# Moving half of a factor's sums into the end of the attention, and tying the residual adds to later products

## The chip, the cores and the metric

The kernel is one program for a Trainium2 chip and uses one of its cores. Its engines are TensorE (PE, matrix products, with the weight loads PEld), VectorE (DVE), ScalarE (ACT), GpSimd (POOL) and SyncE (SP, which here only starts transfers). Each works through its own queue of instructions in order and waits on semaphores for the others; transfers can be started from SP, ACT and POOL. PSUM is the memory that PE writes its results to, SBUF the working memory; DRAM holds the inputs, the outputs and intermediate results.

The metric is the device time of one execution in microseconds (us), the median of several runs. A profiled execution gives a trace beside it.

## The reference

Attention and a feed-forward network run side by side on the normalised input, and both are added to it. All is float32.

```python
def reference(x, Wq, Wk, Wv, Wo, w1_w, w1_s, w2_w, w2_s, h1_w, h1_s, h2_w, h2_s, w3_w, w3_s):
    # x: 2 x 2048 x 256; W*: 256 x 256; the *_w hold -1, 0 and 1, the *_s a scale for each output
    xn = layernorm(x)
    return x + attn(xn, Wq, Wk, Wv, Wo) + ffn(xn, ...)

def attn(x, ...):           # one head, causal, scores scaled by 256 ** -0.5
    return softmax(mask(x @ Wq @ (x @ Wk).T / 16)) @ (x @ Wv) @ Wo

def ffn(x, ...):            # tlin(x, w, s) = (x @ w.T) * s
    h = silu(tlin(x, w1_w, w1_s)) * tlin(x, w2_w, w2_s)     # 256 -> 1024
    h = gelu(tlin(h, h1_w, h1_s))                           # 1024 -> 1024
    h = gelu(tlin(h, h2_w, h2_s))                           # 1024 -> 1024
    return tlin(h, w3_w, w3_s)                              # 1024 -> 256
```

## The kernel before

**Blocks and precision.** The 4096 tokens make N = 8 blocks of TB = 512, blocks 0 to 3 of the first sequence and 4 to 7 of the second (NB = 4); a block has NT = 4 tiles of P = 128 rows. A float32 value goes into PE as a sum of two parts, high and low. `split_into` makes them: the high part is a rounding copy on ACT (L187), the low part a subtraction on DVE (L188).

**Attention.** It runs first. Row tiles (n, t) are taken in the order j = 0 to 31, sequence one from its last tile down, then sequence two upwards. Of each tile the scores are made (PE L425, moved out of PSUM by DVE L434, exponential on ACT L446), turned (DVE L308, to DRAM as d, back as e, both by SP), split into high and low parts pT (ACT L484; L486 on DVE, or on POOL for odd key blocks) and used to weigh the values (PE L518 and L523). The results r go to DRAM as `r_d`. The tiles of x lie in a pool `xp` of four buffers of 512 KB; for the second sequence they are last read when keys are made in the steps j = 13 to 24. `beside(cost)` is called between the steps and drops small pieces of other work among them (`looks`: loads of weights on ACT's queue, checks, the sums of the first square layer's factors on DVE).

**Feed-forward network** (`ffn_ternary`). It follows and works on pairs of blocks (n, n + 1). `first(n)` makes the gated layer: the products (PE L174), silu on ACT (L182), the second factor on DVE (L183). The two square layers, "h1" and "h2", are done as a Strassen-Winograd scheme: the hidden width is halved and the two blocks of the pair are the other half, so that seven products take the place of eight. `STEPS` names them, weight factor and right side:

```python
STEPS = [("A11", "B11"), ("S1", "T1"), ("S2", "T2"), ("S4", "B22"), ("S3", "T3"), ("A12", "B21"), ("A22", "T4")]
```

Each product is 32 matmuls (L883) of some 0.227 us. The right sides are sums of what the layer before gave, made in four chunks: T1 (L858) and T2 (L864) on DVE, the source of T3 (L863) and of T4 (L922) on POOL; each is then split. In the trace T1 and T2 are `h_T`, B22 is `h_B`, T3 is `q`, and the later B21 and T4 are `h_h_B` and `h_h_T` in the first layer of the first pair. L894 copies and L903 and L904 add up and apply gelu to what products left in the banks `ps` and `ps_own`.

**Factors.** The seven weight factors of a layer lie in DRAM (`factors`), and `fetch_factors` (SP, L998, 1 MB each) keeps three of them loaded ahead. A11, A12 and A22 are parts of the weights, S1 to S4 are sums of them, made by the kernel in four chunks. Those of h1 are made in the attention. Those of h2 are made while the first pair goes through the gated layer and its first square layer: `fetch_h2(c)` loads chunk c into one of two staging buffers (SP, L957), `make_h2(c)` makes its four sums in place on POOL (L963 to L966, 128x512 each) and stores them (POOL's queue, L967, 1 MB). `later` says at which point of the program each stands: fetches of chunks 0 and 1 ahead of everything, `make_h2(0)` and `make_h2(1)` in the gated layer, the fetches of chunks 2 and 3 there too, their sums behind products 2 and 3. `copy_h2` copies the unsummed parts from DRAM to DRAM, and `load_w3` (product 5) loads the last weights and rounds them on POOL.

**Residuals.** `rests_of(n)`, called behind product 3 of the second square layer, loads r and x of both blocks (SP L1013 and L1014) into the staging buffers and adds them on POOL, one add of 128x1024 for each block (L1015). The last product of the pair (PE L1044), its scaling and the store follow.

**What sets the order.** A scheduler in the tile framework lays the instructions of each engine in an order of its own from dependences, buffers and estimated times; program order is only a start. `tc.issue_after(mark)` tells it to place an instruction behind another in this plan; it is no data dependence.

Of the kernel before, what the change touches and what calls it, by code (L numbers as in the profile page):

```python
# [30 lines left out]
LEAST = 5  # L31
TURN_KEYS = [8, 10, 12, 14]
LOOKS_FROM = 3
LEAD = 2
# [31 lines left out]
def attn_ffn_kernel(  # L66
# [77 lines left out]
    def sums_of_factors(sums, halves, which, engine=nc.gpsimd):  # L144

        (a11, a21), (a12, a22) = ((t[:, :HB], t[:, HB:]) for t in halves)
        done = sums.bitcast(F32) if sums.dtype == F32R else sums
        for i in which:
            x, y, op = (
                (a21, a22, ALU.add),  # L150
                (done[:, 0, :], a11, ALU.subtract),
                (a12, done[:, 1, :], ALU.subtract),
                (a11, a21, ALU.subtract),
            )[i]
            engine.tensor_tensor(sums[:, i, :], x, y, op)


# [33 lines left out]
    with ExitStack() as actx:  # L191
# [476 lines left out]
        for i, (srcs, steps) in enumerate(items):  # L668
# [7 lines left out]
            if not nxt and i + 1 < len(items):  # L676
                looks.append((4000, lambda i=i: fetched_weights(i + 1)))

        since = [0]

        def beside(cost):
            if j >= LOOKS_FROM:
                since[0] += cost
                if looks and since[0] >= looks[0][0]:
                    since[0] = 0
                    looks.pop(0)[1]()
# [75 lines left out]
        while until < len(tiles) - 1:  # L762
# [16 lines left out]
            merged(a, b, beside)  # L779

        last_quarter = [bank(), bank()]
        with tc.issue_after(marks["PE"]):
            gated_products(last_quarter, xh0, HK - 1)

    def ffn_ternary(actx):
# [83 lines left out]
        def square(layer, n, B, sets, last, beside):  # L869
# [6 lines left out]
            def product(step, out, start):  # L876
# [3 lines left out]
                for o in range(HK):  # L880
                    for c in range(HK):
                        for a in range(2):
                            nc.tensor.matmul(  # L883
                                out=out[o], lhsT=w[:, c, ts(o, P)], rhs=sets[right][c][:, a, :],
                                start=(start and c == 0 and a == 0), stop=(c == HK - 1 and a == 1),
                                skip_group_check=True,
                            )
                if step in beside:
# [57 lines left out]
            return C, nxt  # L946

        raw_h2 = {}

# [9 lines left out]
        def make_h2(c):  # L959

            t = raw_h2.pop(c)
            a11, a21, a12, a22 = (t[:, i, :] for i in range(4))
            nc.gpsimd.tensor_tensor(a22, a21, a22, ALU.add)  # L963
            nc.gpsimd.tensor_tensor(a21, a11, a21, ALU.subtract)
            nc.gpsimd.tensor_tensor(a11, a22, a11, ALU.subtract)
            nc.gpsimd.tensor_tensor(a12, a12, a11, ALU.subtract)  # L966
            nc.gpsimd.dma_start(out=factors["h2"][:, 1:5, c, :], in_=t)  # L967
# [7 lines left out]
        def copy_h2(step):  # L975
# [4 lines left out]

        later = {
            "B11": lambda: make_h2(0), "B21": lambda: (make_h2(1), copy_h2(0)), "B12": lambda: fetch_h2(2),
            "B22": lambda: fetch_h2(3), 0: lambda: copy_h2(5),
            2: lambda: (make_h2(2), copy_h2(6)), 3: lambda: make_h2(3), 5: load_w3,
# [19 lines left out]
        def rests_of(n):  # L1004
# [4 lines left out]
            )  # L1009
            rests = {}  # L1010
            for i, m in enumerate((n + 1, n)):
                rests[m] = rest = rt[:, ts(i, NT), :]
                nc.sync.dma_start(out=rest, in_=r_d[m].rearrange("p (t d) -> p t d", d=D))  # L1013
                nc.sync.dma_start(out=xt[:, ts(i, NT), :], in_=rows_of(m))  # L1014
                nc.gpsimd.tensor_tensor(rest, rest, xt[:, ts(i, NT), :], ALU.add)  # L1015
            return rests

        load_xh(1)
        for c in range(2):
            fetch_h2(c)  # L1020
        fetch_factors()

        for n in range(0, N, 2):
# [6 lines left out]
            B, sets = square("h1", n, B, sets, False, later)  # L1030
            rests = {}
            B, sets = square("h2", n, B, sets, True, {3: lambda: rests.update(rests_of(n))})
            for m in (n + 1, n):
# [221 lines left out]
```

## Time and profile before

| | us |
|---|---|
| median of 3 runs | 869.92 |
| lowest and highest | 867.67, 871.22 |
| the profiled execution | 868.75 |
| its span in the trace | 866.9 |
| PE busy | 849.5 |
| DVE busy | 644.1 |
| ACT busy | 498.7 |
| POOL busy | 234.7 |

Of the profiled execution 1.85 us lie around the span. Mean granted clock of PE: 0.998. The feed-forward part starts at about 281 us, and the first pair's first square layer runs from 302 to 354.

In timelines a row is: start in us, duration in us, engine, line, operation, output <- inputs (names without buffer numbers), shape, count, and in brackets the idle time before it and who ended that. Rows of windows give, for each engine, busy us and instructions, in the order PE, PEld, DVE, ACT, POOL, then the granted clock of PE as a share of full speed, the busy share of the DMA engines, and GB/s.

### The profile page before, as it was taken

To read this page: it belongs to the slowest core of one execution; us is meant where nothing else is said; L and a number is where in the kernel's file an instruction comes from. 1 tells how busy PE (TensorE), PEld (TensorE's weight loads), DVE (VectorE), ACT (ScalarE), POOL (GpSimd) and SP (SyncE) were. 2 spreads that over 40 slices of the span, in tenths; PEclk is the share of its full clock that TensorE was granted. 3 is DMA by queue.
4 is the path that set the end of the run, shared out by engine and by line. 5 is a ranking of instruction groups with operands and counts; after the bars stand their busy time and mean duration, and the time that the engine had idled before them with its cause. 6 is when DMAs were issued, how large, how long until landed. Compare 5 with 4: busy or idle time off the path is not lost.

```text
span 866.9 us, 12257 instructions
## 1 busy us (share of the span) xinstructions
PE 849.5 (98%) x4298; PEld 720.5 (83%) x4298; DVE 644.1 (74%) x1123; ACT 498.7 (58%) x881; POOL 234.7 (27%) x178
## 2 busy tenths in 40 slices
PE   9999799999999999999999999999999999999997
PEld 7988688988888878878988888988888898888887
DVE  6689685887965799986596596479478648848764
ACT  3456665655655466676257576436557635557671
POOL 3022823111111666630142150026024003502300
PEclk9999999999999999999999999999999999999999
DMA  8987899667881998754234444433444431144411
GB/s 276 361 233 233 249 314 291 222 234 231 286 283 51 389 403 282 285 194 152 93 132 143 144 146 141 144 116 109 145 145 145 145 135 58 49 146 146 146 49 53
DMA packets 62678, 162.51 MB, mean 187 GB/s; under 512 B 6545, under 2 KB 36369, under 8 KB 53265
## 3 DMA queue, kind: packets, MB, share of 16 engines
q1 hardware_dynamic: 57792, 145.14, 48.6%
q10 hardware_dynamic: 3728, 12.32, 4.6%
q0 software_dynamic: 1088, 4.19, 1.3%
q8 instruction: 36, 0.59, 0.3%
q14 instruction: 34, 0.27, 0.1%
HBM read 120.21 MB, written 47.71 MB: 194 GB/s over the span
## 4 chain that ended last, share of the span: by engine, by line
PE 83%; DVE 6%; DMA 5%; issue 2%; POOL 1%; ACT 1%; SPq 1%; DVEq 0%; ACTq 0%; POOLq 0%
PE ps_own L883 22%; PE ps L883 21%; PE ps L425 7%; PE ps L174 6%; PE ps_own L174 6%; PE po L518 4%; PE ps_own L1044 4%; PE ps L1044 4%; PE ps L398 3%; DMA e<-d 3%; DMA d<-b 2%; PE po L523 2%; PE ps L382 1%; POOL x L345 1%; DVE h_T L188 1%
## 5 line engine op out<-in xcount | busy, mean ns | idle before, releaser
L425 PE MATMUL ps<-k,q 128*128 128x512 f32 (+3 forms) x480 | 109.0, 366 | 0.4 <-ACT q L264 0.4
L425 PEld LDWEIGHTS ps<-k,q 128*128 128x128 f32 x480 | 82.0, 189 | 13.4 <-ACT q L264 1.2
L518 PE MATMUL po<-v,pT 128*128 128x512 f32 x272 | 79.1, 401 | 6.5 <-ACT pT L484 4.7
L486 POOL TENSOR_TENSOR pT<-e,pT 128x512 fp32r<-128x512 f32 (+3 forms) x30 | 36.8, 1229 | 140.1 <-ACT pT L484 102.6
L1015 POOL TENSOR_TENSOR rt<-rt,xt 128x1024 f32<-128x1024 f32 x8 | 21.9, 2758 | 170.3 <-issue 114.8
L904 ACT ACTIVATE k_h_u<-k_h_u,h_s_sb 128x512 f32<-128x512 f32 x64 | 45.9, 723 | 36.6 <-DVE k_h_u L903 36.0
L446 ACT ACTIVATE s<-s,low 128x1024 f32<-128x1024 f32 (+7 forms) x48 | 42.9, 895 | 30.8 <-DVE low L440 30.6
L518 PEld LDWEIGHTS po<-v,pT 128*128 128x128 f32 x272 | 47.3, 189 | 14.3 <-ACT pT L484 5.5
L863 POOL TENSOR_TENSOR k_h_u<-k_h_p,k_h_u 128x512 f32<-128x512 f32 x16 | 23.3, 1459 | 122.1 <-ACT q L187 106.0
L484 ACT CAST pT<-e 128x512 fp32r<-128x512 f32 (+3 forms) x60 | 32.8, 574 | 38.8 <-DMA e<-d 26.9
L434 DVE TENSOR_SCALAR_CACHE_REDUCE s<-ps 128x512 f32<-128x512 f32 (+3 forms) x80 | 47.2, 598 | 5.0 <-PE pt L490 3.1
L523 PEld LDWEIGHTS po<-v,pT 128*128 128x128 f32 x272 | 42.4, 188 | 6.8 <-DVE pT L486 0.7
L523 PE MATMUL po<-v,pT 128*128 128x256 f32 x272 | 46.2, 283 | 0.1
L188 DVE TENSOR_TENSOR q<-k_h_u,q 128x512 fp32r<-128x512 f32 x32 | 43.4, 1384 | 0.0
L308 DVE STREAM_TRANSPOSE b<-s 128x1024 f32<-128x1024 f32 (+3 forms) x30 | 33.4, 1124 | 8.3 <-ACT s L446 4.8
L922 POOL TENSOR_TENSOR k_h_p<-f_h_B,k_h_p 128x512 f32<-128x512 f32 x16 | 32.6, 2065 | 20.0 <-DVE h_h_T L188 20.0
L174 PE MATMUL ps<-xh,w_sb 128*128 128x512 f32 x144 | 36.4, 391 | 0.8 <-ACT b L182 0.8
L863 POOL TENSOR_TENSOR f_w_B<-f_w_B,f_w_B 128x512 f32<-128x512 f32 x16 | 26.8, 1692 | 33.1 <-DVE f_w_B L183 33.1
L903 DVE TENSOR_TENSOR k_h_u<-ps_own,k_h_u 128x512 f32<-128x512 f32 x32 | 21.7, 686 | 17.5 <-PE ps_own L883 17.4
L904 ACT ACTIVATE k_h_p<-k_h_p,h_s_sb 128x512 f32<-128x512 f32 x32 | 22.8, 722 | 19.3 <-DVE k_h_p L903 19.3
L903 DVE TENSOR_TENSOR k_h_u<-ps,k_h_u 128x512 f32<-128x512 f32 x32 | 22.0, 690 | 14.3 <-PE ps L883 14.3
L174 PE MATMUL ps<-xh1t,w_sb 128*128 128x512 f32 x128 | 31.8, 389 | 0.0
(178 smaller groups left out, 2206.2 us busy)
## 6 DMA issues: line engine op xcount, KB each, us to landing
w_h_S<-factors_h SPq DMA_DIRECT2D x32, 1024.0 KB, 4.8
w_h_A<-factors_h SPq DMA_DIRECT2D x24, 1024.0 KB, 4.8
d<-b SPq DMA_DIRECT2D x18, 512.0 KB, 3.9
e<-d SPq DMA_DIRECT2D x72, 128.0 KB, 3.2
xT_d<-k SPq DMA_DIRECT2D x8, 1024.0 KB, 6.0
stg<-in_ffn_h_w ACTq DMA_DIRECT2D x16, 512.0 KB, 4.8
r_d<-r SPq DMA_DIRECT2D x8, 512.0 KB, 4.3
factors_h<-xh SPq DMA_DIRECT2D x4, 1024.0 KB, 4.5
```

Of the source, the lines that this page charges most:

```text
L174: nc.tensor.matmul(out=p, lhsT=w[:, c, ts(o, P)], rhs=xh[:, c, a, :], start=(c == 0 and a == 0), stop=(c == DC - 1 and a == 1),)
L188: nc.vector.tensor_tensor(r[:, 1, :], f, r[:, 0, :].bitcast(F32), ALU.subtract)
L425: nc.tensor.matmul(out=ps[:, :w], lhsT=qs[n][:, c, a, ts(t, P)], rhs=ks[m][:, c, b, :w], start=(k == 0), stop=(m < n and k == 3 * DC - 1),)
L434: marks["DVE"] = nc.vector.tensor_scalar(st["s"][:, ds(at, w)], ps[:, :w], 1.0, None, ALU.mult, ALU.max, accum_out=st["tops"][:, m - first ...
L446: marks["ACT"] = nc.scalar.activation(st["s"][:, at], st["s"][:, at], AF.Exp, bias=low, accum_out=st["sums"][:, u // UK : u // UK + 1],).ins
L518: nc.tensor.matmul(out=st["po"], lhsT=pT[:, 0, ts(j, P)], rhs=vs[m][:, j, :, :], start=(m == first and j == 0), stop=False,)
L523: marks["PE"] = nc.tensor.matmul(out=st["po"][:, 0, :], lhsT=pT[:, 1, ts(j, P)], rhs=vs[m][:, j, 0, :], start=False, stop=(m == n and j == ...
L863: nc.gpsimd.tensor_tensor(B["B12"][i], B["B22"][i], B["B12"][i], ALU.subtract)
L883: nc.tensor.matmul(out=out[o], lhsT=w[:, c, ts(o, P)], rhs=sets[right][c][:, a, :], start=(start and c == 0 and a == 0), stop=(c == HK - 1 ...
L903: nc.vector.tensor_tensor(r[o], banks[o], r[o], ALU.add)
L904: nc.scalar.activation(C[k][o], r[o] if r else banks[o], AF.Gelu, scale=s[:, at : at + 1])
L1044: nc.tensor.matmul(out=ys[t][:, :D], lhsT=h[c][:, a, ts(t, P)], rhs=w3_sb[:, c, :], start=(c == 0 and a == 0), stop=(c == HC - 1 and a == 1),)
```

## The change

Chunks 0 and 1 of h2's factor sums are made in the attention from tile j = 24 on: their weights are loaded into x's four buffers on ACT's queue, the eight sums are made one at a time on POOL between the attention's steps, and four stores of 512 KB follow on POOL's queue. The feed-forward part loads chunks 2 and 3 at its start, behind `xh1` and the first three factors. The residual adds are cut from two of 128x1024 to eight of 128x256 for each pair and are built inside `tc.issue_after` of the last matmul of product 3 (block n + 1) and product 4 (block n). The number and size of the sums stays the same.

```diff
+RAWS_FROM = 24
+EARLY = 2
...
+    def sums_in_place(halves):
+        a11, a21, a12, a22 = halves
+        return (
+            (a22, a21, a22, ALU.add), (a21, a11, a21, ALU.subtract),
+            (a11, a22, a11, ALU.subtract), (a12, a12, a11, ALU.subtract),
+        )
...
+        raws = {}
+        def fetch_raws(c):
+            raws[c] = [xp.tile([P, 2, HB], F32, tag="x", name=f"raw_h2_{c}_{i}") for i in range(2)]
+            for t, k in zip(raws[c], (c, c + HK)):
+                with tc.issue_after(marks["ACT"]):
+                    nc.scalar.dma_start(out=t, in_=h2[:, k, :].rearrange("p (i o) -> p i o", i=2))
+        def sum_raws(c, i):
+            with tc.issue_after(marks["DVE"]):
+                nc.gpsimd.tensor_tensor(*sums_in_place([t[:, k, :] for t in raws[c] for k in range(2)])[i])
+        def store_raws(c):
+            for i, t in enumerate(raws[c]):
+                nc.gpsimd.dma_start(out=factors["h2"][:, 1 + 2 * i : 3 + 2 * i, c, :], in_=t)
+        made_of_h2 = [(0, lambda c=c: fetch_raws(c)) for c in range(EARLY)]
+        for c in range(EARLY):
+            made_of_h2 += [(9000, lambda c=c, i=i: sum_raws(c, i)) for i in range(4)]
+            made_of_h2.append((4000, lambda c=c: store_raws(c)))
+        since_made = [0]
         def beside(cost):
+            if j >= RAWS_FROM:
+                since_made[0] += cost
+                if made_of_h2 and since_made[0] >= made_of_h2[0][0]:
+                    since_made[0] = 0
+                    made_of_h2.pop(0)[1]()
...
-                            nc.tensor.matmul(
+                            marks["PE"] = nc.tensor.matmul(
...
-                            )
+                            ).ins
...
-            a11, a21, a12, a22 = (t[:, i, :] for i in range(4))
-            nc.gpsimd.tensor_tensor(a22, a21, a22, ALU.add)
-            nc.gpsimd.tensor_tensor(a21, a11, a21, ALU.subtract)
-            nc.gpsimd.tensor_tensor(a11, a22, a11, ALU.subtract)
-            nc.gpsimd.tensor_tensor(a12, a12, a11, ALU.subtract)
+            for k in sums_in_place([t[:, i, :] for i in range(4)]):
+                nc.gpsimd.tensor_tensor(*k)
...
         later = {
-            "B11": lambda: make_h2(0), "B21": lambda: (make_h2(1), copy_h2(0)), "B12": lambda: fetch_h2(2),
-            "B22": lambda: fetch_h2(3), 0: lambda: copy_h2(5),
+            "B21": lambda: copy_h2(0), 0: lambda: copy_h2(5),
             2: lambda: (make_h2(2), copy_h2(6)), 3: lambda: make_h2(3), 5: load_w3,
         }
...
-                nc.gpsimd.tensor_tensor(rest, rest, xt[:, ts(i, NT), :], ALU.add)
-            return rests
+                adds[m] = [(r, r, xt[:, i * NT + t, :], ALU.add) for t in range(NT) for r in [rest[:, t, :]]]
+            return rests, adds
+        def add_rests(adds):
+            for k in adds:
+                with tc.issue_after(marks["PE"]):
+                    nc.gpsimd.tensor_tensor(*k)
         load_xh(1)
-        for c in range(2):
+        fetch_factors()
+        for c in range(EARLY, HK):
             fetch_h2(c)
-        fetch_factors()
...
-            rests = {}
-            B, sets = square("h2", n, B, sets, True, {3: lambda: rests.update(rests_of(n))})
+            rests, adds = {}, {}
+            def fetch_rests():
+                for a, b in zip((rests, adds), rests_of(n)):
+                    a.update(b)
+                add_rests(adds[n + 1])
+            B, sets = square("h2", n, B, sets, True, {3: fetch_rests, 4: lambda: add_rests(adds[n])})
```

More of the change, by code (lines that the diff above doesn't have):

```diff
@@ L779, in attn_ffn_kernel @@
             merged(a, b, beside)
+        assert not made_of_h2
         last_quarter = [bank(), bank()]
@@ L946, in square @@
             return C, nxt
+        marks = {}
         raw_h2 = {}
@@ L1030, in ffn_ternary @@
             B, sets = square("h1", n, B, sets, False, later)
-            rests = {}
-            B, sets = square("h2", n, B, sets, True, {3: lambda: rests.update(rests_of(n))})
+            rests, adds = {}, {}
+            def fetch_rests():
[3 more added lines that the diff above has]
+            B, sets = square("h2", n, B, sets, True, {3: fetch_rests, 4: lambda: add_rests(adds[n])})
             for m in (n + 1, n):
```

## The prediction

> **What bounds the kernel now.** The first view is the page's list of engines, the second its chain of waits by engine:
>
> ```profile
> PE 849.5 (98%) x4298; PEld 720.5 (83%) x4298; DVE 644.1 (74%) x1123; ACT 498.7 (58%) x881; POOL 234.7 (27%) x178
> ...
> PE 83%; DVE 6%; DMA 5%; issue 2%; POOL 1%; ACT 1%; SPq 1%; DVEq 0%; ACTq 0%; POOLq 0%
> ```
>
> TensorE (PE) is busy 98% of the span. The change neither adds nor removes a matmul, so it can only win back PE's waits or lengthen them. The third view lists those waits (us in total, times, longest):
>
> ```profile
> PE po L518 <- ACT pT L484: 4.7, 2, 2.6
> ...
> PE ps_own L883 <- DVE h_h_T L188: 1.4, 2, 1.0
> ...
> PE ps L174 <- ACT b L182: 0.8, 1, 0.8
> PE ps L883 <- DVE h_T L188: 0.7, 1, 0.7
> ...
> PE ps L883 <- DVE f_w_B L183: 0.3, 1, 0.3
> ```
>
> The first lies at 87 and 103 us, long before anything that the change touches. The rest is the prize. Taken as start-to-start gaps above the usual 0.227 us of a matmul they are 0.92 us at 261 (end of the attention), 0.41 at 307 and 0.85 at 318 (first pair, first square layer), 0.59 and 1.13 at 370 (second square layer). All of them together are 3.9 us of 867, so little can be won.
>
> The fourth view is the timeline of the first square layer, where the change moves most: PE, then VectorE (DVE), then GpSimd (POOL).
>
> ```profile
> 309.78 7.43 PE L883 MATMUL ps_own<-h_T,w_h_S 128*128 128x512 f32 x32
> 317.04 1.75 PE L883 MATMUL ps<-h_T,w_h_S 128*128 128x512 f32 x7
> 319.48 5.96 PE L883 MATMUL ps<-h_T,w_h_S 128*128 128x512 f32 x25 [0.69 <-DVE h_T L188]
> ```
>
> ```profile
> 316.44 2.98 DVE L188 TENSOR_TENSOR h_T<-f_w_B,h_T 128x512 fp32r<-128x512 f32 x3
> 319.35 4.69 DVE L188 TENSOR_TENSOR q<-f_w_B,q 128x512 fp32r<-128x512 f32 x4
> ...
> 329.67 7.21 DVE L188 TENSOR_TENSOR h_h_T<-f_w_B,h_h_T 128x512 fp32r<-128x512 f32 x4
> ...
> 379.09 2.48 DVE L188 TENSOR_TENSOR h_h_T<-k_h_p,h_h_T 128x512 fp32r<-128x512 f32 x4
> ```
>
> ```profile
> 317.20 5.09 POOL L922 TENSOR_TENSOR f_w_B<-f_w_B,f_w_B 128x512 f32<-128x512 f32 x3 [1.23 <-DVE h_T L188]
> 324.00 1.79 POOL L963 TENSOR_TENSOR stgt_h<-stgt_h 128x512 f32<-128x512 f32 x1 [1.71 <-DMA stgt_h<-in_ffn_h_w]
> ```
>
> Product 2 (its right side T2) ran 7 matmuls and waited until 319.42, when DVE had split the last chunk of T2 (the third h_T). Two readings carry the forecast. First, a DVE subtraction with both operands in SBUF takes 2.48/4 = 0.62 us when POOL is idle (at 379) and 7.21/4 = 1.80 us while POOL adds (at 329, beside the sums of L963). POOL next to it needs 5.09/3 = 1.70 us an operation. So DVE and POOL take turns: in a stretch where both have such work, one pair costs 1.70 us and DVE loses 1.1 us to each POOL operation. DVE's products from PSUM (L183, 0.74 us) show no such stretch. Second, T2 was only 0.85 us late, so any POOL operation set ahead of it on this path costs 1.1 us of PE.
>
> **Part 1, the first square layer.** Before, the sums of chunks 0 and 1 (8 POOL operations) ran from 288.9 to 302, those of chunks 2 and 3 from 324 on, after T2. After, chunks 0 and 1 are gone from here, but chunks 2 and 3 come from the first fetch of this stage, and in the built order their 8 sums are mixed with the four L863 (T3's source) and the first three L922 (T4's source), ahead of T2's last split. On DVE the order changes too: L188 of T2's chunk 3 now stands behind all four splits of T3 (q); before, T2's four came first. L922 of a chunk waits for T2's split of it, so POOL's delays and DVE's feed each other.
>
> When the sums start: SP issues its first transfer here at 280.5. The new queue is xh1t, three factor loads and chunk 2, 5.24 MB. This window carries
>
> ```profile
> 289.00:296.00 7.00, 7.00 (x32) 5.80 (x31) 5.95 (x7) 3.37 (x6) 6.84 (x5) 1.00 1.02 423
> ```
>
> 423 GB/s at a full DMA share (last two columns), so 12.4 us, and with some 3 us from issue to the first landing chunk 2 is there at 296. DVE then has 19 subtractions with both operands in SBUF up to and with T2's chunk 3 (the rest of T1, four splits of B22, four L864, four of T2, four of T3), POOL 15 operations. 15 pairs of 1.70 and four DVE operations alone at 0.60 are 27.9 us: from 296.9 to 324.8, where before PE went on at 319.5. That is **+5.3 us**. The same count over the old order (from 303.0: 7 POOL operations, 14 of DVE) gives 303.0 + 11.9 + 4.2 = 319.1 against 319.42 measured. Bounds: 1.80 a pair and six alone give 327.5 (+8); chunk 2 at 293, as chunk 1 landed before, and pairs partly apart give 321.5 (+2). PE would wait twice, some 2 us for T2's chunk 2 and some 3 to 5 us for chunk 3.
>
> Such waits can cost more than themselves. PE's timeline has one in the attention, and the row of windows behind it shows the clock:
>
> ```profile
> 138.44 1.19 PE L518 MATMUL po<-v,pT 128*128 128x512 f32 x3 [1.89 <-DVE r L537]
> ```
>
> ```profile
> 139.00:142.40 3.40, 3.40 (x16) 3.02 (x15) 1.88 (x6) 2.26 (x5) 0.00 (x0) 0.50 0.99 282
> ```
>
> After a wait of 1.89 us the granted clock (third column from the end) was 0.50 for 3.4 us; twelve matmuls of L398 took 2.88 us in it where their count at full clock is 1.54, so about 1.5 us were lost. After the waits of 2.2 and 2.6 us at 87 and 103 us there was no drop: one case in three. Two waits by 1/3 by 1.5 us: **+1.0** (0 to +3). [...]
>
> **Part 2, the second square layer.** PE's two waits at 370 (0.59 and 1.13) come from T2 there, split while POOL made the two adds of 128x1024 at 358.8 and 367.1; DVE's operation beside each took 2.9 us. After, this pair's adds stand in POOL's order right behind the rounding of w3 and ahead of L863 of this layer. Their rows can land by about 339 (SP's queue: r behind the rounding, x behind a factor load that is free when product 2 ends), so they are over near 345, and L863 is needed at 346 plus the 5 us that PE is later. The two waits go: **-1.7** (0 if the adds hold L863 up). Next late there is nothing: T2 gains 2 x 2.2 us against a lateness of 1.7.
>
> **Part 3, the adds cut in eight.** Two of 2758 ns become eight of 128x256. POOL's rows of that shape are 652 ns (L345, one input) and 1252 ns (L486), so 5.2 to 10 us against 5.5; I take the middle, as either way it is off the path: in later pairs POOL has been idle for tens of us before them. POOL's order holds no wait for PE at these adds, only for their rows, so "released by later products" sets a place in the queue and no time. Price **0** (-0.5 to +1).
>
> **Part 4, the attention's end.** Four loads of 512 KB on ACT's queue come at 187 to 190, and eight sums (1.3 to 1.7 us) and four stores (0.81 each, before two) on POOL between 196 and 210. In 190 to 195 the DMA share is 1.01 at 380 GB/s already, in 195 to 201 it is 0.90. 2.1 MB at 380 GB/s is 5.5 us, of which 0.6 find room: rows of e can come up to 4.9 us late. PE's order has scores put ahead of the weighing that needs them. Queued behind the sums on POOL is the low part of tile (5,2)'s pT: it is written at some 211.3, and PE asks for it at about 212. Five or so of DVE's operations lose 1.1 us there while it must clear score banks. I take 2.1 us lost (0 to 4.9), nearer to the low end because PE has a tile's scores in hand, less the 0.9 at 261, which the order of loads ahead of it can close: **+1.2** (-0.9 to +4).
>
> **Sum.** 5.3 + 1.0 - 1.7 + 0 + 1.2 = **+5.8 us**. On the profiled execution (868.75, span 866.9 and 1.85 around it) that is 874.6; that execution is 1.17 below the median of 869.92, so the median becomes **875.7**.
>
> **Rivals.**
> - A, not slower: POOL is free from the stage's start to 296 and only four DVE operations fall in that time today beside sums; if chunk 2 lands late enough, or T2's last split is written before PE's 7th matmul of product 2 at 317.9, all waits there and at 370 go: 0.85 + 0.41 + 1.72 = 3.0 us, 866.9. For it: eight POOL operations have left before 302. Against: 15 are queued ahead of T2's end instead of 7. It decides on whether POOL's sums run ahead of L863 or slip behind L922. Chance 0.22.
> - B, the attention's end is hit: e's rows come the whole 4.9 us late and POOL's pT after 213, 4 to 6 us on top, 880.5. For it: DMA share of 1.01. Against: 0.7 us of margin on pT. Chance 0.13.
> - C, the adds hold up L863 of the second layer: instead of -1.7 a wait of 1 to 3 us, 877 to 880. It decides if their rows land after 345. Chance 0.08, counted in the forecast's upper part.
>
> **How the numbers follow.** The forecast has 0.65. 0.5% is 4.35 us, about what a measurement of this kernel can tell from no change. Of the forecast's 0.65 about a quarter lies below +4.35 (its T2 term at +2 to +4); B is slower wholly; A is within the bound but for 0.04 of it. So faster 0.04, same 0.35, slower 0.61. The range runs from 868.0 (most of A's side left out) to 881.5 (T2's +8 with the attention at its value, or B). The forecast's own is 871.5 to 879.5.
>
> **What would show it.** Right: in the changed trace PE waits 5 to 7 us in all within product 2 of the first pair's first layer, for L188 of h_T; DVE's SBUF subtractions take 1.7 us from about 296 to 323; POOL's sums begin near 296; no PE wait in the second layer's T2. Possibly a row of granted clock 0.50 follows the wait. Wrong: that wait under 2 us, chunk 2 there before 293, or new PE waits of over 4 us between 190 and 262.

## The result, and the profile after

The change makes the kernel slower: 883.59 us (median of four executions, 880.12 to 885.69) against 868.79 for the kernel before in the same series, a ratio of 1.016 (95% interval 1.0132 to 1.0189). A second series, told below, gave 879.24 against 867.64, 1.0126 (1.0086 to 1.0165). So the cost is 11 to 15 us. 875.7 was forecast, with a range up to 881.5: the direction was right, and the forecast loss of 5.8 us is 40 to 50% of the measured one. The first series lies 2.1 us above the range, the second inside it. Further down, a bracket such as (1.016, 1.0132 to 1.0189) holds the ratio to the kernel before in the same series and its interval.

The profiled execution after took 880.12 us, span 878.3. The page's engines and its chain of waits:

```profile
PE 853.5 (97%) x4298; PEld 722.9 (82%) x4298; DVE 641.7 (73%) x1123; ACT 501.2 (57%) x881; POOL 241.6 (28%) x204
...
PE 70%; DMA 13%; DVE 10%; ACT 3%; issue 3%; SPq 1%; POOL 0%; DVEq 0%; ACTq 0%
```

PE's busy time rose by 4.0 us with the same 4298 matmuls, so part of the loss is not waiting but slower matmuls: the clock was at half in some stretches, and a matmul alone between two waits took 0.50 us (both below). In the chain DMA went from 5% to 13%. PE's waits:

```profile
PE po L528 <- ACT pT L494: 7.8, 4, 2.5
PE ps L922 <- DVE h_T L198: 4.6, 3, 2.2
...
PE ps L922 <- ACT h_T L197: 1.5, 2, 0.7
```

(L528 is L518 of before, L922 is L883, L198 and L197 are L188 and L187.) The wait of the second square layer for `h_h_T` is gone, the one for T2 (`h_T`) has become 6.1 us, and the attention's wait for pT went from 4.7 to 7.8 (the 4.7 and half of the 7.8 lie at 86 to 107 us, ahead of what the change touches).

To put a place to each microsecond, take the time between the starts of fixed matmuls in PE's order: 1000 to 1560 is the attention's end, 1560 to 1800 holds product 2 of the first square layer, 1800 to 2000 the first products of the second layer, 2000 to 4290 all the rest. Every kernel below does the same PE work in each (one profile each, us):

| kernel | attention's end | product 2's stretch | second layer | rest |
|---|---|---|---|---|
| before | 105.4 | 56.0 | 47.3 | 466.4 |
| after | 109.2 | 64.0 | 45.3 | 465.5 |
| after, second series (f4) | 112.8 | 64.6 | 45.3 | 465.6 |

After loses 3.8 to 7.4 us at the attention's end and 8.0 to 8.6 around product 2, and wins 2.0 in the second layer and 0.8 to 0.9 in the later pairs: 9 to 13 us. (Both profiles of after were also 2.1 us later at matmul 1000. From the first matmul to that one the kernels told here took 182.3 to 188.8 us, kernels without the change among the shortest and the longest, so I take these 2.1 us as variation.)

**Product 2** in PE's timeline after, to be held against the prediction's three lines:

```profile
322.36 0.84 PE L922 MATMUL ps<-h_T,w_h_S 128*128 128x512 f32 x3
323.55 0.50 PE L922 MATMUL ps<-h_T,w_h_S 128*128 128x512 f32 x1 [0.35 <-DVE h_T L198]
324.80 0.50 PE L922 MATMUL ps<-h_T,w_h_S 128*128 128x512 f32 x1 [0.75 <-ACT h_T L197]
327.51 0.50 PE L922 MATMUL ps<-h_T,w_h_S 128*128 128x512 f32 x1 [2.21 <-DVE h_T L198]
328.76 0.80 PE L922 MATMUL ps<-h_T,w_h_S 128*128 128x512 f32 x1 [0.75 <-ACT h_T L197]
331.60 7.81 PE L922 MATMUL ps<-h_T,w_h_S 128*128 128x512 f32 x25 [2.04 <-DVE h_T L198]
```

Five waits, 6.10 us in all: for the low part (L198) of T2's chunk 1 and for the high (L197) and low parts of chunks 2 and 3. DVE and POOL at that time:

```profile
314.72 5.66 DVE L198 TENSOR_TENSOR h_B<-f_w_B,h_B 128x512 fp32r<-128x512 f32 x2
...
327.38 0.68 DVE L903 TENSOR_TENSOR f_w_B<-f_w_B,b 128x512 f32<-128x512 f32 x1
327.98 2.96 DVE L198 TENSOR_TENSOR q<-f_w_B,q 128x512 fp32r<-128x512 f32 x3
330.86 0.68 DVE L198 TENSOR_TENSOR h_T<-f_w_B,h_T 128x512 fp32r<-128x512 f32 x1
```

```profile
301.98 8.19 POOL L1003 TENSOR_TENSOR stgt_h<-stgt_h 128x512 f32<-128x512 f32 x5 [26.14 <-DMA stgt_h<-in_ffn_h_w]
...
316.04 1.30 POOL L902 TENSOR_TENSOR f_w_B<-f_w_B,f_w_B 128x512 f32<-128x512 f32 x1
317.28 1.30 POOL L1003 TENSOR_TENSOR stgt_h<-stgt_h 128x512 f32<-128x512 f32 x1
318.53 1.28 POOL L902 TENSOR_TENSOR f_w_B<-f_w_B,f_w_B 128x512 f32<-128x512 f32 x1
```

POOL's sums (L1003, the former L963 to L966) start at 302.0, which is 296.1 in the time of the profile before (after is 5.9 us later by then): the chunk landed when it was forecast to. T2's last split ends at 331.54, 325.6 in that time, against 324.8 forecast. What was not in the sum follows in the windows (granted clock third from the end):

```profile
323.00:329.00 6.00, 1.94 (x5) 0.80 (x4) 6.00 (x6) 3.69 (x8) 4.79 (x3) 0.97 0.52 180
328.70:332.10 3.40, 1.30 (x2) 0.79 (x3) 3.40 (x6) 3.40 (x9) 1.67 (x3) 0.50 0.98 414
332.10:335.50 3.40, 3.40 (x9) 2.63 (x8) 3.40 (x4) 1.12 (x3) 3.40 (x3) 0.50 0.66 270
```

PE was busy 1.94 of 6 us, and then had half the clock for 6.8 us; in the second half of these it had no wait left.

**The attention's end.** PE waits there twice that it did not before, at 199 and at 258 us, both times for a high part of pT, whose rows of e came late. The DMA view of after and then of before, in the few microseconds in which the rows for the first wait were issued (count, KB each, median us to landing):

```profile
e<-d SPq DMA_DIRECT2D x3, 96.0 KB, 7.4
```

```profile
e<-d SPq DMA_DIRECT2D x3, 96.0 KB, 4.6
```

In after these three rows were issued at 187.9 to 189.4 us, among the first three of the four new loads of 512 KB (188.2, 188.6 and 189.8). The second wait, in the chain of after:

```profile
245.56 0.32 SPq L626
...
248.71 9.24 DMA e<-d
...
258.77 1.19 PE po L528 x4
```

L626 on SP is the load of `xh0`, 1 MB, old work, which in the new order of the attention's steps is issued right ahead of four rows of e; two loads of 512 KB on ACT's queue (the check of w3) are issued around it. In the kernel before the same three loads came at 237 to 241 us and the next four rows were issued at 249.9 to 251.2 and took 2.9 us. So the change has delayed rows of e more than 50 us after its own loads were issued, through the order that the scheduler made around its steps.

### The profile page after: what moved, and what is told of

Its sections match the earlier page's. It is cut to its first block, busy times and chain, and to the rows that moved or that the text cites. A ratio compares the mean times of both kernels' runs of the same rounds, so it can differ in the third digit from the quotient of the medians.

```text
span 878.3 us, 12287 instructions
## 1 busy us (share of the span) xinstructions
PE 853.5 (97%) x4298; PEld 722.9 (82%) x4298; DVE 641.7 (73%) x1123; ACT 501.2 (57%) x881; POOL 241.6 (28%) x204
## 4 chain that ended last, share of the span: by engine, by line
PE 70%; DMA 13%; DVE 10%; ACT 3%; issue 3%; SPq 1%; POOL 0%; DVEq 0%; ACTq 0%
PE ps L922 22%; PE ps_own L922 22%; PE ps L184 7%; PE ps_own L184 6%; DMA d<-b 4%; DMA e<-d 4%; PE ps_own L1092 3%; PE ps L1092 3%; DVE s L444 2%; DMA stg<-in_ffn_h_w 2%; PE po L528 1%; DVE b L318 1%; DMA factors_h<-xh 1%; PE ps L408 1%; DMA r_d<-r 1%
## 5 line engine op out<-in xcount | busy, mean ns | idle before, releaser
L528 PE MATMUL po<-v,pT 128*128 128x512 f32 x272 | 80.3, 407 | 7.9 <-ACT pT L494 7.8
L1058 POOL TENSOR_TENSOR rt<-rt,xt 128x256 f32<-128x256 f32 x32 | 27.5, 899 | 183.9 <-issue 115.2
L528 PEld LDWEIGHTS po<-v,pT 128*128 128x128 f32 x272 | 48.5, 194 | 16.5 <-ACT pT L494 9.8
L902 POOL TENSOR_TENSOR k_h_u<-k_h_p,k_h_u 128x512 f32<-128x512 f32 x16 | 23.2, 1452 | 124.1 <-ACT q L197 106.1
L533 PEld LDWEIGHTS po<-v,pT 128*128 128x128 f32 x272 | 43.0, 194 | 9.2 <-DVE pT L496 3.5
L198 DVE TENSOR_TENSOR q<-k_h_u,q 128x512 fp32r<-128x512 f32 x32 | 44.8, 1428 | 0.0
L961 POOL TENSOR_TENSOR k_h_p<-f_h_B,k_h_p 128x512 f32<-128x512 f32 x16 | 34.4, 2180 | 21.8 <-DVE h_h_T L198 21.8
L922 PE MATMUL ps<-h_T,w_h_S 128*128 128x512 f32 x128 | 33.2, 413 | 6.1 <-DVE h_T L198 4.6
L496 DVE TENSOR_TENSOR pT<-e,pT 128x512 fp32r<-128x512 f32 x30 | 26.7, 889 | 14.9 <-ACT pT L494 14.8
L922 PEld LDWEIGHTS ps<-h_T,w_h_S 128*128 128x128 f32 x128 | 25.4, 199 | 13.3 <-DVE h_T L198 5.8
```

What stands on the lines that cost most here:

```text
L198: nc.vector.tensor_tensor(r[:, 1, :], f, r[:, 0, :].bitcast(F32), ALU.subtract)
L496: engine.tensor_tensor(lo, src, hi.bitcast(F32), ALU.subtract)
L528: nc.tensor.matmul(out=st["po"], lhsT=pT[:, 0, ts(j, P)], rhs=vs[m][:, j, :, :], start=(m == first and j == 0), stop=False,)
L533: marks["PE"] = nc.tensor.matmul(out=st["po"][:, 0, :], lhsT=pT[:, 1, ts(j, P)], rhs=vs[m][:, j, 0, :], start=False, stop=(m == n and j == ...
L922: marks["PE"] = nc.tensor.matmul(out=out[o], lhsT=w[:, c, ts(o, P)], rhs=sets[right][c][:, a, :], start=(start and c == 0 and a == 0), sto ...
```

## The experiments

**1. What makes product 2 late.** Four kernels in one series (before: 868.63). Their expectations in us count from the 883.6 of the first series.

e10: in the changed kernel, DVE's splits of T3 are placed behind T2's last one (`low_of["T2"]`). POOL's order is the same.

```diff
...
+            low_of["T2"] = low_of["last"]
...
-            sets["T3"] = [split_into(h_views[i], B["B12"][i]) for i in range(HK)]
+            with tc.issue_after(low_of["T2"]):
+                sets["T3"] = [split_into(h_views[i], B["B12"][i]) for i in range(HK)]
```

> The changed kernel with one edit: on DVE the four splits of T3 (q) are placed behind the last split of T2. POOL's order stays. In the changed kernel product 2 lost 9.6 us to waits and the clock drop behind them, in the kernel before 1.5. Theory 'order on DVE': the four q splits ahead of T2's last chunk make most of that; without them product 2 loses 3 us or less and the time falls by 6 to 8 us to about 876. Theory 'sums on POOL': L864 of chunk 3 is late already because POOL's sums stand ahead of it, q takes only about 4 us of it, and product 2 still loses about 5 us: about 879.

Four waits are left in product 2, 3.92 us in all; the two longest:

```profile
322.48 0.50 PE L925 MATMUL ps<-h_T,w_h_S 128*128 128x512 f32 x1 [1.31 <-ACT h_T L199]
325.85 0.79 PE L925 MATMUL ps<-h_T,w_h_S 128*128 128x512 f32 x1 [1.84 <-ACT h_T L199]
```

Product 2's stretch took 62.0 us, 2.0 to 2.6 less than after, and 7.6 above the 54.4 that e6 will show it to take without a wait. The time, 875.96 (1.0089, 1.0055 to 1.0122), is what the first theory gave, but product 2 lost 7.6 us and not its 3 or less; the attention's end of 108.4 us is part of the fall in time. So DVE's order is a fifth to a quarter of the loss of product 2, and e6 tells what the rest is.

e6: the eight sums of chunks 2 and 3 and their two stores stand on POOL behind the last L922 of the layer, not among L863 and L922.

```diff
-                nc.gpsimd.tensor_tensor(t4, B["B21"][i], t4, ALU.subtract)
+                marks["T4"] = nc.gpsimd.tensor_tensor(t4, B["B21"][i], t4, ALU.subtract).ins
...
-            for k in sums_in_place([t[:, i, :] for i in range(4)]):
-                nc.gpsimd.tensor_tensor(*k)
-            nc.gpsimd.dma_start(out=factors["h2"][:, 1:5, c, :], in_=t)
+            with tc.issue_after(marks["T4"]):
+                for k in sums_in_place([t[:, i, :] for i in range(4)]):
+                    nc.gpsimd.tensor_tensor(*k)
+                nc.gpsimd.dma_start(out=factors["h2"][:, 1:5, c, :], in_=t)
```

> The changed kernel with one edit: the eight sums of chunks 2 and 3 and their stores are placed on POOL behind the four L922 of the first square layer, instead of among L863 and L922. Theory 'sums on POOL': no POOL sum is ahead of T2, product 2 loses under 1 us, and the time falls by 8 to 9 us to about 875. Rival 'the loads': product 2 is late for another reason (factor loads or PSUM banks) and at least 4 us of the loss stay: 879 or more.

The whole of product 2 in one row of PE's timeline, with no wait:

```profile
319.70 7.42 PE L922 MATMUL ps<-h_T,w_h_S 128*128 128x512 f32 x32
```

54.4 us, 1.6 below the kernel before, and 871.12 (1.0039, 1.0012 to 1.0065). So POOL's sums ahead of T2, with the splits of DVE that they hold up, are the whole loss of product 2, half clock included. In the second layer a wait of 0.96 came back (46.9 us), as its adds now stand among its L863.

e1: in the changed kernel, chunks 2 and 3 are loaded ahead of the three factors.

```diff
-        fetch_factors()
         for c in range(EARLY, HK):
             fetch_h2(c)
+        fetch_factors()
```

> The changed kernel with one edit: chunks 2 and 3 are loaded ahead of the first three factors, as chunks 0 and 1 were before. Theory 'the place of the load': the sums run from about 293 to 307 in the changed kernel's time, ahead of L863, so product 2 loses 1 to 2 us and the time falls by 7 to 8 us to about 876. Rival 'eight sums ahead of T2 cost the same wherever they stand': product 2 still loses 6 us or more, 880 or more.

Seven matmuls, one wait, as in the kernel before:

```profile
322.77 5.96 PE L922 MATMUL ps<-h_T,w_h_S 128*128 128x512 f32 x25 [0.73 <-DVE h_T L198]
```

55.6 us and 870.54 (1.0006, 0.9982 to 1.003): the order of two groups of loads at the start of the stage takes back nearly all of the change's cost. The sums ran from 292.3 to 305, in a time in which a good part of DVE's work comes from PSUM (with POOL at work beside it such a product took 0.74 us in after, at 314.06); the four subtractions beside them that took 1.7 to 2.1 us came well ahead of T2's splits.

e3: the same edit the other way round, on the kernel before, with nothing moved into the attention.

> The kernel before with one edit: the first three factors are loaded ahead of chunks 0 and 1; nothing is moved into the attention. Theory 'the place of the load': its eight sums meet L863 and L922 as in the changed kernel, product 2 loses 7 to 9 us and the time is 875 to 877 against 869. Rival 'the loss of product 2 needs what the attention now does': 869 to 871.

```profile
PE ps L883 <- DVE h_T L188: 4.9, 3, 2.2
...
PE ps L883 <- ACT h_T L187: 1.2, 2, 0.8
```

The five waits of after are here too, 6.1 us; the stretch took 65.3 us and the kernel 876.00 (1.0083, 1.0046 to 1.012). The place of the load alone makes the loss of product 2; the attention has no part in it.

**2. The change once more.**

> The changed kernel itself once more, beside the others. Its stages in the first profile (attention's end +3.8 us, product 2 +8.0, second layer -2.0, later pairs -0.8) sum to +9, which would be 877 to 879 on the kernel before; its first four executions had a median of 883.6. If the stages are the whole effect: 877 to 879. If something in them varies from one execution to the next that the one profile missed (PE's waits or the clock drop in product 2): 882 to 885, and a second profile with another length in one of these stages.

879.24 us in this series, so the median is what the stages of the first profile give; the profile fell on the slowest of its four executions (884.21) and does show another length in one stage. Product 2 lost much the same (64.6), the attention's end 3.6 us more. Its waits there were 2.80 and 2.17 us against the first profile's 1.48 and 2.41, 1.1 more in all, and each was followed by a half-clock window:

```profile
200.50:203.90 3.40, 3.40 (x10) 2.62 (x9) 3.40 (x12) 2.53 (x6) 3.26 (x3) 0.51 0.96 346
...
262.00:265.40 3.40, 3.40 (x13) 2.91 (x12) 2.71 (x8) 3.00 (x8) 0.26 (x1) 0.50 0.75 245
```

So a stage with waits of 2 to 3 us has no one price: it differs from one execution to the next (109.2 and 112.8 us here) by the windows that it draws. What went ahead of a window can be read from the profiles. In after, f4 and before windows began whole steps of 3.41 us apart (last section). The wait of 2.41 in after left PE 1.66 of 3.43 us busy in its step, and no window followed; that of 2.17 in f4 left it 1.25 of 3.42, and one did:

```profile
257.00:260.43 3.43, 1.66 (x9) 1.45 (x10) 1.68 (x4) 2.23 (x5) 0.46 (x1) 1.00 0.69 238
```

```profile
258.55:261.97 3.42, 1.25 (x6) 0.97 (x6) 1.17 (x3) 1.82 (x4) 0.47 (x1) 1.00 0.80 282
```

**3. What the attention pays for.** All on e1, whose attention is that of the change; its end took 109.9 us there (before: 105.4). One profile is a weak measure of it: with PE's order of the change the end took 107.1 to 112.8 us in seven profiles (h2, f3, e10, e6, after, e1, f4; mean 109.2), with the order of before 104.2 to 106.9 in six (h1, before, k2, e7, e4, e3; mean 105.7). So the attention pays some 3.5 us, and a difference of 2 us between two profiles tells little.

f1 leaves out the eight sums, f2 the four loads (POOL fills the buffers instead, four operations of 0.9 us):

> The kernel with the chunks loaded first (e1), with the eight sums of the attention left out: chunks 0 and 1 are loaded and stored unsummed. From the 1000th matmul to the 1560th (end of the attention) the kernel before takes 105.4 us, e1 109.9. Theory 'the loads delay the rows of e': 108.5 to 110 here too, about 870. Rival 'POOL's sums delay pT and DVE': 105.5 to 107, about 867.

> The kernel with the chunks loaded first (e1), with the four loads of 512 KB in the attention left out: the buffers are filled with a constant on POOL instead, the eight sums and four stores follow as before. Same stretch: theory 'the loads delay the rows of e': 105.5 to 107 us, about 867. Rival 'POOL's sums delay pT and DVE': 109 to 111, as POOL has four fills more, 870 to 871.

f1: 110.0 us, 871.12 (1.0049, 1.0029 to 1.007). f2: 111.0 us, 872.47 (1.0068, 1.0039 to 1.0096). Neither theory holds alone: both lie above all six profiles with PE's order and attention of before, so neither edit took the price away, and what each half costs is not told apart by one profile of each. In f1 a wait of 2.07 for pT at 200 stayed (rows of e 8 to 9 us in flight). In f2, whose order on PE is that of the kernel before, PE waited elsewhere, for DVE's moves of scores out of PSUM, and a half-clock window followed (206.5 to 209.9 us). The waits of f2, then DVE's timeline:

```profile
PE ps L435 <- DVE s L444: 3.0, 2, 2.8
```

```profile
205.24 1.01 DVE L496 TENSOR_TENSOR pT<-e,pT 128x512 fp32r<-128x512 f32 x1 [4.08 <-ACT pT L494]
```

The scores stood on DVE's queue behind a split of pT that waited for rows of e. In the kernel before these four rows were issued at 195.1 to 196.3, ahead of two old loads of 512 KB (197.3), and took 3.1 to 4.5 us. In f2 they were issued at 196.9 to 198.4, behind these loads (196.4), and took 6.1 to 6.4. POOL ran its sums from 188.7 on and DVE was busy throughout 187 to 195, so it is likely that the sums held up the turn that the rows wait for; that link was not tried by itself. f1's order on PE differs from both, so its number holds loads and order together.

g2 spreads the loads over the steps and puts the sums later:

```diff
+GAP = 10000
+SUM_GAP = 7000
...
-        made_of_h2 = [(0, lambda c=c: fetch_raws(c)) for c in range(EARLY)]
+        made_of_h2 = [(GAP, lambda c=c, i=i: fetch_raws(c, i)) for c in range(EARLY) for i in range(2)]
...
-            made_of_h2 += [(9000, lambda c=c, i=i: sum_raws(c, i)) for i in range(4)]
+            made_of_h2 += [(SUM_GAP, lambda c=c, i=i: sum_raws(c, i)) for i in range(4)]
```

> The kernel with the chunks loaded first (e1), with the attention's four raw loads spread over its steps and the eight sums and four stores later and closer together (gaps 10000 and 7000 instead of 0 and 9000). From the 1000th to the 1560th matmul: before 105.4, e1 109.9. Theory 'four loads at once delay the rows of e at 190 to 198 and with them PE at 197': that wait (0.9 to 3 us in the kernels so far) is under 0.5 us, and the stretch takes 106 to 108. Rival 'any place costs the same': 109 to 111.

The wait at 197 went, as expected, but the stretch grew to 113.0 and the time to 877.66 (1.0089, 1.0066 to 1.0111). The new wait is for POOL's own queue, in which the low part of pT stood behind the sums (a half-clock window followed, 222.9 to 226.3 us):

```profile
PE po L535 <- POOL pT L498: 2.7, 1, 2.7
```

g3 leaves out the attention's check of w3, the two loads around `xh0`:

> The kernel with the chunks loaded first (e1), with the attention's check of w3 left out: its two loads of 512 KB on ACT's queue and the operations on them, which in e1 and the changed kernel stand with the 1 MB load of xh0 ahead of four rows of e that landed after 8 to 11 us (2.6 in the kernel before). Theory 'the wait of PE at 253 to 258 (1.3 to 2.6 us) is these 2 MB ahead of e': with half of them gone the rows land within 6 us and the wait is under 1 us. Rival 'PE has lost its lead by then through POOL's sums and the first wait': the wait stays at 1.3 us or more.

The wait at 253 to 258 went; the four rows of e took 6.0 to 7.9 us instead of 8 to 11, and another wait of 0.85 for pT appeared at 264. So that wait goes with these loads in front of e, though PE's order changed a little too, so that its lead is not ruled out. The end took 107.7 us, which is within the spread above, and the time was 871.13 (1.0019, 1.0002 to 1.0036).

**4. The residual adds.**

f3: e1 with the adds of before, two of 128x1024:

> The kernel with the chunks loaded first (e1), with the residual adds as they were: two of 128x1024 for each pair, no issue_after. In the built order they stand at the same place, ahead of L863 of the second layer. Theory 'their place comes from the earlier loads, not from the edit': no wait in product 2 of the second layer, 45.3 us from the 1800th to the 2000th matmul (47.3 before), 870 to 871. Rival 'the cut into eight and the later products take the wait away': 47 us there and about 872.5.

```profile
334.80 4.75 POOL L1051 TENSOR_TENSOR rt<-rt,xt 128x1024 f32<-128x1024 f32 x2 [5.95 <-issue]
```

45.3 us in the second layer and 868.53 (1.0014, 0.9991 to 1.0038): the two large adds are over at 339.6, 7 us before L863 (here L902) begins at 347.0, without any edit of the adds. Their rows come earlier since the chunks left the staging buffers earlier: the first load of r is issued as the last store of a chunk has landed, at 315.2 us here and at 344.1 before.

e4: the adds' edit alone, on the kernel before, one execution:

> The kernel before with the change's edit of the residual adds alone: eight of 128x256 for each pair, built inside issue_after of products 3 and 4. In POOL's built order the two groups of four stand where the two adds of 128x1024 stood, one ahead of and one behind the first L922 of the second layer. If the edit moves nothing: the second layer's product 2 waits as before, 47 us or a little more from the 1800th to the 2000th matmul, 868 to 870. If its wait on later products is real: 45.3.

The adds did not move, as POOL's timeline shows, with L922 between them:

```profile
364.30 4.62 POOL L1023 TENSOR_TENSOR rt<-rt,xt 128x256 f32<-128x256 f32 x4
371.96 1.68 POOL L922 TENSOR_TENSOR k_h_p<-f_h_B,k_h_p 128x512 f32<-128x512 f32 x1 [3.04 <-DVE h_h_T L188]
373.60 4.63 POOL L1023 TENSOR_TENSOR rt<-rt,xt 128x256 f32<-128x256 f32 x4
```

Yet the second layer took 45.8 us, not the 47 expected, with one wait of 0.17 left of the two of 0.43 and 0.96. The cut does something that its place does not: DVE's operations beside adds of 1.15 us took 1.2 us (1.22 and 1.23 at 367.10 and 368.24), where in the kernel before the one beside an add of 2.94 took 2.88, at 359.44 (the time of one execution, 872.27, tells nothing). The later pairs show it too: 465.6 us in the rest with eight adds (e1, e4), 466.3 and 466.4 with two in the same place (f3, before).

e7: the two large adds stay, but behind the L922 on POOL's own queue.

> The kernel before with one edit: the residual adds stay two of 128x1024 for each pair, but are placed on POOL behind the four L922 of the second square layer by an issue_after of the last of them, on POOL's own queue. No change elsewhere. Theory 'POOL's adds beside T2's splits are the whole wait of the second layer': no wait in product 2 there (45.3 us from the 1800th to the 2000th matmul instead of 47.3), 2 us less, 865.7 to 867 beside 868. Rival 'the splits are late for L922 and L864 alone': 46.5 to 47.3, no difference.

45.3 us, as expected, and 465.4 in the rest; the time, for which 2 us less was expected, is 870.44 against 870.38 (0.9993, 0.9976 to 1.0009). 2 us are within that interval, so the gain is seen in the profile and not shown in the time.

**5. A version that beats both?** Three kernels put together what had helped, without the loss of product 2.

> The kernel before with two edits: chunk 1's sums are placed on POOL behind the four L922 too, with those of chunks 2 and 3 after them (chunk 3 is loaded after product 2), so that only chunk 0's four sums run ahead of T2; and the residual adds stand behind the L922 of the second layer as in e7. Nothing is moved into the attention. Theory 'every POOL sum ahead of T2 costs product 2': 54.5 us from the 1560th to the 1800th matmul (56.0 before, 54.4 in e6), 45.3 in the second layer, 3 us less than the kernel before: 865 to 867 beside 868 to 870. Rival 'the later stores hold up the second layer's factor loads': 46 us or more in the second layer, no gain.

> The kernel with the sums behind T4 (e6), with the residual adds placed behind the L922 of the second layer as well. Product 2 and the second layer should then lose nothing: 54.4 and 45.3 us, together 3.6 less than the kernel before, and what remains is the attention's price of 3 to 5.5 us (108.5 to 111 us from the 1000th to the 1560th matmul): 0 to 2 us more than the kernel before. If the attention's price were only in the order of that profile: 2 to 3 us less than the kernel before.

> h1 with one edit: the first two sums of chunk 1 are placed among the L863 (behind the second and the third of them) instead of behind the L922, so that chunk 1's store, chunk 3's load and chunk 3's store come some 3.4 us earlier. In h1 chunk 3's store landed at 352.7 and the factor load that waits for it at 359.3, 1.9 us after PE wanted it. If that store is the wait: the load lands at 356, PE does not wait in the second layer (45.3 us), product 2 keeps 54.4 to 54.9, and the time is 864 to 866 beside 868. If the two sums cost T2 what sums ahead of it cost elsewhere (1.1 us each with no slack): 56 us in product 2 and no gain over h1.

h1: 54.4 us in product 2's stretch, as expected, but 49.4 in the second layer, as its rival had it: 867.79 (1.0004, 0.9987 to 1.0021). PE waited for a factor whose load stood behind chunk 3's store, and ran at half clock for 3.4 us behind that (from 359.6):

```profile
PE ps L883 <- DMA w_h_S<-factors_h: 1.9, 1, 1.9
```

k2 removed that wait only to have DVE's split of q late, and product 2's old wait back (0.70; before 0.69): 55.4 and 47.4 us, 867.67 (1.0006, 0.9993 to 1.0019). The split of q stood behind a subtraction that began as POOL issued chunk 3's store and lasted until POOL's next three operations were done:

```profile
PE ps_own L885 <- DVE q L188: 1.3, 2, 0.9
```

```profile
348.82 4.50 DVE L188 TENSOR_TENSOR h_h_T<-k_h_u,h_h_T 128x512 fp32r<-128x512 f32 x1
```

h2: 54.4 and 45.6 us, 107.1 at the attention's end: 869.41 (1.0032, 1.0009 to 1.0054). It has taken 3.3 us off these two stages. Its profile, at 865.61 one of its quickest executions, pays back only 1.7 in the attention; the median is 1.8 us above the kernel before, and which stage makes that up was not seen. None of them beats the kernel before.

## Why the prediction was right or wrong

- **Product 2's lateness: right.** The stretch had 6.10 us of waits against 0.94 before, 5.2 more where the count of pairs gave 5.3; the chunk came at 296.1, the last split at 325.6 against 324.8. e3, e1 and e6 show the cause (the chunks behind the factors, POOL's sums ahead of T2), and e10 the part of DVE's order. That the numbers agree so closely is in part luck: in that time DVE had 20 such subtractions and four products from PSUM besides, where the count had 19 subtractions alone; POOL's 15 operations cost it 1.0 us each instead of 1.1 (29.6 us less 14.6 for DVE's work alone); and one subtraction did not take turns at all (last section).
- **The term that failed there is the clock and the restarts: +1.0 forecast.** The stretch lost 8.0 to 8.6 us with 5.2 and 4.9 us more of waits, so they cost 2.9 to 3.8. The price was taken as one chance in three after each of two waits. In fact there were five waits close together (four in e10), and half clock followed in each kernel that had them: 6.8 us of it in after and e10, 10.2 in f4 and e3. The longest gap does not tell them apart: here it was 2.21, and f4's 2.17 and 2.80 were followed by a window too, while 2.41 at 258 in after was not. PE's busy share of the 3.41 us ahead does so in these: 0.15 ahead of after's window in product 2, 0.18 and 0.37 ahead of f4's in the attention, 0.49 at 258 in after (one case that it does not tell is in the last section).
- **The attention's term failed: +1.2 forecast, 3.8 and 7.4 in the two profiles of after, 3.5 in the mean of all.** The value was placed at the low end "because PE has a tile's scores in hand". The rows of e at 188 came 2.8 us late in after and 4.9 in f4, where the sum's upper bound had 4.9, and PE did wait. And there are two such delays where the sum had one: the step that it left out is that the new pieces shift the old ones, so that the loads of `xh0` and w3 came in front of rows of e at 246, which took 10.5 us instead of 2.9. The half-clock windows behind these waits were priced nowhere. The prediction's own sign of being wrong, new waits of over 4 us between 190 and 262, was just missed in after (3.89) and met in f4 (4.97).
- **The second layer: right in size (-1.7 forecast, -2.0), and by the step given.** f3 shows the place, e4 (one execution) that the cut alone would have done most of it; the prediction gave the cut no part. Rival C, the adds in front of L863, did not come: in after they are over at 353.1 and L863 begins at 359.7.
- **"Released by later products" is nothing on the chip: right.** In e4 the adds stand where they stood. But the price of the cut was not 0: it gains 0.7 us in the later pairs (e1 against f3, e4 against before).
- **Rival A** (all waits gone) did not come. Of the two places that it named, POOL's sums ahead of L863 are what e1 makes true, and product 2 then is nearly where it was (55.6, before 56.0); the sums behind L922 are e6, and there the waits of product 2 did go (54.4). **Rival B** named the rows of e, which was so, and pT on POOL, which was in time here (g2 is where it was not).

The two failed terms were 1.9 to 2.8 and 2.6 to 6.2 us too small; the second layer and the later pairs gave back 1.1. The medians lie 9.0 and 5.8 us beyond the forecast's +5.8 in the two series; single executions of the changed kernel spread over 9 us.

## What to carry to other kernels

When work is moved to another stage, cost both ends by the queue that it joins: what stands behind it on that queue, what its transfers stand in front of, and what old work is shifted into a new neighbour. Moving a load behind others can cost more than the work that was moved away: here the place of two chunks' loads in SP's queue decides 7 us in the kernel before (e3) and some 10 in the changed one (e1). Several short waits close together are to be priced with a slow clock behind them (four or five of them in product 2 were followed by 6.8 to 10.2 us at half clock in after, f4, e10 and e3), and a profile of one execution gives only one draw of that. The attention's price stays in part open: neither its loads nor its sums alone account for it.

## What the runs showed of the hardware

**DVE beside POOL.** In after one DVE subtraction did not take turns with POOL at all. The row at 314.72 above holds it: it began at 315.77, 0.53 us after POOL's issue of a transfer (0.77 us), and lasted 4.61 us, through all of POOL's next three operations, which ran at 1.30, 1.30 and 1.28 us, near L863's shortest time in before (1.28 us at 345.78). It had begun 0.27 us ahead of the first of them and ended 0.57 us behind the last; why it did not get its turn in between is not shown. f4 holds such a subtraction too (its row of two at 318.39 took 5.65 us, that of after 5.66), as does e10 with 4.60, and k2 with the 4.50 above. Elsewhere the turns agree only roughly: a pair took 1.70 us (before, POOL at 317.20), where 0.62 (DVE at 379 in before, with POOL idle) and 1.30 add up to 1.92.

**Half-clock windows.** In after they began at 89.77, 123.90, 328.70 and 874.83 us, 10, 60 and 160 steps of 3.413 us apart, in f4 at 200.50, 262.00 and 330.20, 18 and 20 steps apart, and in before at 138.99 and 866.03, 213 steps apart. The table has the steps ahead of these windows, and the emptiest steps at full clock in before and after that had none behind them:

| profile | step, us | PE busy, share of the step | clock in the next step |
|---|---|---|---|
| before | 862.62 to 866.03 | 0.00 | 0.50 |
| after | 325.29 to 328.70 | 0.15 | 0.50 |
| f4 | 197.09 to 200.50 | 0.18 | 0.51 |
| after | 86.35 to 89.77 | 0.28 | 0.50 |
| f4 | 327.00 to 330.20 (3.20 us of it) | 0.31 | 0.50 |
| after | 871.42 to 874.83 | 0.33 | 0.50 |
| f4 | 258.55 to 261.97 | 0.37 | 0.50 |
| before | 135.58 to 138.99 | 0.45 | 0.50 |
| before | 101.45 to 104.86 | 0.49 | 1.00 |
| after | 257.02 to 260.43 | 0.49 | 1.00 |
| after | 120.49 to 123.90 | 0.64 | 0.50 |

So in these the share ahead of a window was 0.45 or less but for one case at 0.64. From 328.70 on in after PE was busy 0.38 of the first step at half clock, and the second was at half clock too; in that one it was busy throughout, and full clock followed at 335.53.

**Rows of e.** With little else under way a row of 128 KB landed after 2.6 to 3.0 us (before, issued from 249.91 to 251.22; the DMA engines moved 0 to 29 GB/s from 249.5 to 251.0). Rows of 80 KB landed after 9.2 to 11.4 us where the load of `xh0` on SP's queue and two of 512 KB on ACT's, 2 MB in all, were issued around them (after, at 245 to 249), and after 7.3 us in the median with `xh0` and without these two (g3, issued at 241 to 245).
